# Cross-attention setup: weight and context transposes moved ahead of products on TensorE, block transposes moved ahead of copies on VectorE

## The chip, the cores and the metric

The kernel runs on one core of a Trainium2 chip. The metric is device time in microseconds for one execution. Three runs of the kernel before gave 283.92, 284.35 and 285.65 us, so the median is 284.35 us.

## The reference

One layer of cross-attention, in float32, with 16 batches, 256 queries of width 256, 77 keys of width 192 and 8 heads of width 256:

```
Q = (x @ Wq)   K = (c @ Wk)   V = (c @ Wv)      # split into 8 heads of 256
score = Q K^T / sqrt(256), masked
ctx   = softmax(score) V
out   = ctx @ Wo + x
return layernorm(out) * gamma + beta
```

x is 16 x 256 x 256, c is 16 x 77 x 192, Wq is 256 x 2048, Wk and Wv are 192 x 2048, Wo is 2048 x 256.

## The kernel before

**What it computes instead.** The kernel never forms Q and K. Per head it makes G = Wk Wq^T / 16 once (192 x 256), then A = c G for each batch, and the scores are x A^T. In the same way it makes U = Wv Wo per head once and uses c U in place of V Wo. The 192 rows of Wk and of c are split into 128 (names ending in A: gA, cA, uA) and 64 (gB, cB, uB).

**Order.** The kernel is scheduled by hand: on every engine the instructions stand in the order in which the Python code emits them, and an engine waits where its next instruction isn't ready. There is no planner.

**The setup**, lines 547 to 827, comes before a loop over the batches (line 838). In order of the code:

1. SP issues the loads (lines 574 to 601). The order on its queue is: wk_nat first half, wk_last, wq_nat first half, wk_nat second half, wq_nat second half, the first three row blocks of the context c_sb (load_c(0, first), where first is 3), then the block-wise weights wk_blk and wq_blk for e = 0 and e = 1, the rest of c_sb, wvT, wo, the mask and x.
2. keep_busy (line 606) runs transposes of an identity matrix on TensorE that nothing reads.
3. Half of the heads goes through TensorE transposes. turn_k(e) and turn_q(e, u) (lines 625 to 637) transpose four 128 x 128 chunks each into one PSUM bank, pt, and one copy takes the bank to SBUF (kT, qT). g_of(e) (line 721) multiplies kT and qT into a bank pg, which ScalarE scales into gA. rest_of_g(u) (line 735) does the 64 remaining rows into a bank ph, which VectorE scales into gB.
4. turn_c (line 654) transposes row blocks of the context on TensorE into banks pc and copies them to cA and cB; GpSimd copies cB to the other half of the partitions.
5. turn_blk(e) (line 647) transposes the other half of the heads' weights on VectorE, in 32 x 32 blocks, with one instruction for kT_blk and one for qT_blk. of_pair and rest_of_pairs (lines 679 and 691) multiply these into the banks pgb and phb.
6. a_of_places (line 749) makes A for the first four batches. Its products (lines 199 and 213) fill all eight banks of PSUM (pa), and eight copies take them to SBUF (a).
7. The rest of the setup makes U (banks pu and pw), the bias from the mask, transposed x, and the last 13 keys (banks pr).

**Copies.** evacuate (line 148) gives odd calls to ScalarE and even calls to VectorE, counted over the whole kernel:

```
evacs[0] += 1
if evacs[0] % 2:
    nc.scalar.copy(dst, src)
else:
    nc.vector.tensor_copy(dst, src)
```

**PSUM.** All banks come from one ring of eight (ps_mm, line 98). A new bank can be written once its earlier content has been read.

**The main loop** (lines 838 to 922) does for each batch the scores (line 313), softmax on VectorE, ScalarE and GpSimd, the products with c U, the residual and the normalisation, and prepares A and c U of later batches.

Of the kernel before, what the change touches and what calls it, by code (L numbers as in the profile page):

```python
# [53 lines left out]
def kernel(  # L54
# [81 lines left out]
    def flat(ap):  # L136
        return ap.rearrange("p a b -> p (a b)")
# [10 lines left out]
    def evacuate(dst, src):  # L148
# [5 lines that stand above are left out]
# [395 lines left out]
    with tc.tile_pool(name="wonce", bufs=1) as wp:  # L549
# [23 lines left out]
        first = -(-GB * S2 // CR)  # L573
# [44 lines left out]
        def turn_chunks(of, name):  # L618

            pt = ps_mm.tile([P, 4, P], F32, tag="mm", name=f"pt_{name}")  # L620
            for i, chunk in enumerate(of):
                nc.tensor.transpose(pt[:, i], chunk, ident)
            return pt

        def turn_q(e, u):
            chunks = [
                wq_nat[:, e, t, u * D + dc * P : u * D + (dc + 1) * P]
                for dc in range(2) for t in range(2)
            ]
            pt = turn_chunks(chunks, f"q_{e}_{u}")  # L630
            evacuate(flat(qT[:, e, u]), flat(pt))

        def turn_k(e):
            pt = turn_chunks([wk_nat[:, e, n * P : (n + 1) * P] for n in range(4)], f"k_{e}")
            evacuate(
                kT[:, e].rearrange("p u n l -> p (u n) l")[:, :, :P], pt
            )
# [9 lines left out]
        def turn_blk(e):  # L647
            for blk, of in ((wk_blk, kT_blk), (wq_blk, qT_blk)):
                nc.vector.transpose(
                    of[:, e].rearrange("p n (m r) -> p m n r", r=BK),  # L650
                    blk[:, e].rearrange("p m (n c) -> p m n c", c=BK),
                )

        def turn_c(lo, hi):
            for r in range(lo, hi, 2):
                n = min(2, hi - r)
                pc = ps_mm.tile([P, 4, P], F32, tag="mm", name=f"pc_{r}")
                for lc in range(2):
                    for j in range(n):
                        nc.tensor.transpose(  # L660
                            pc[:, 2 * lc + j, :CR],
                            c_sb[:, r + j, lc * LB : lc * LB + P],
                            ident[:CR, :CR],
                        )
                rows = slice(r * CR, (r + n) * CR)
                evacuate(flat(cA)[:, rows].rearrange("p (j m) -> p j m", m=CR), pc[:, :n, :CR])
                evacuate(
                    flat(cB)[LB:, rows].rearrange("p (j m) -> p j m", m=CR),
                    pc[LB:, 2 : 2 + n, :CR],
                )  # L670
                nc.gpsimd.tensor_copy(flat(cB)[:LB, rows], flat(cB)[LB:, rows])  # L671
# [34 lines left out]
        def two_banks(name, j):  # L706
            return [ps_mm.tile([P, 2, DI], F32, tag="mm", name=f"{name}_{j}_{e}") for e in range(2)]
# [13 lines left out]
        def g_of(e):  # L721

            pg = ps_mm.tile([P, 2, DI], F32, tag="mm", name=f"pg_{e}")
            for u in range(2):
                for dc in range(2):
                    nc.tensor.matmul(
                        pg[:, u],
                        kT[:, e, u, dc, :P],
                        qT[:, e, u, dc],
                        start=(dc == 0),  # L730
                        stop=(dc == 1),
                    )
            nc.scalar.mul(gA[:, NF * e : NF * e + 2], pg, D ** -0.5)

        def rest_of_g(u):

            ph = ps_mm.tile([P, DI], F32, tag="mm", name=f"ph_{u}")
            for dc in range(2):
                for e in range(2):
                    nc.tensor.matmul(  # L740
                        ph[half(e)],
                        kT[:, e, u, dc, P:],
                        qT[:, e, u, dc],
                        start=(dc == 0),
                        stop=(dc == 1),
                    )
            nc.vector.tensor_scalar(gB[:, u], ph, D ** -0.5, None, ALU.mult)

        def a_of_places(places, between=None):
            part_A, part_B, copies = prepare_a(0, places)  # L750
            part_A()
            part_B()
            for i, (dst, src) in enumerate(copies()):
                evacuate(dst, src)
                if between and i == 3:
                    between()

        turn_k(0)
        keep_busy(2)
# [1 line left out]
        keep_busy(3)  # L761
        turn_q(0, 0)
        turn_q(0, 1)
        g_of(0)
        turn_k(1)
        turn_q(1, 0)
        turn_q(1, 1)
        g_of(1)
        rest_of_g(0)
        rest_of_g(1)  # L770
        turn_c(0, first)
        turn_blk(0)
        a_of_places((0, 1), lambda: turn_blk(1))
        pg = two_banks("pgb", 0)
        for e in range(2):
            of_pair(pg, e, wk_part, wq_part)
# [7 lines left out]
        nc.sync.dma_start(gam, gamma.partition_broadcast(P))  # L784
        nc.sync.dma_start(bet, beta.partition_broadcast(P))
        a_of_places((2, 3))
        turn_v(3)
        turn_c(first, NCR)
# [49 lines left out]
    for b in range(-1, B):  # L838
# [32 lines left out]
        copies = [copy for _, _, of_part in work for copy in of_part()]  # L871
# [94 lines left out]
```

## Time and profile before

| what | value |
|---|---|
| runs | 283.92, 284.35, 285.65 us |
| profiled execution | 285.26 us, span 283.5 us |
| granted TensorE clock, mean | 0.992 |
| TensorE matmul busy | 271.2 us (96% of the span) |
| VectorE busy | 207.5 us (73%) |
| GpSimd busy | 179.6 us (63%) |
| ScalarE busy | 156.8 us (55%) |
| DMA | 22.60 MB, mean 80 GB/s |

The span runs from the first to the last instruction of the profiled execution; its own time is 1.76 us longer. PE is TensorE, PEld its weight loads, DVE VectorE, ACT ScalarE, POOL GpSimd, SP the engine that issues the transfers. "pt L622" is the work that writes tile pt in line 622. A float32 matmul appears as two records and a transpose as one, so that the four products of g_of are "x8" and the four transposes of turn_k "x4". In the chain of work that ended last, each piece is what released the next; "issue" is time in which the engine waited for nothing that the profile shows.

| stage (us from the start) | TensorE busy | VectorE busy | ScalarE busy | GpSimd busy | DMA share |
|---|---|---|---|---|---|
| 0 to 17.34 | 14.40 | 3.58 | 5.31 | 0.79 | 0.90 |
| 17.34 to 58.78 | 41.09 | 24.67 | 10.15 | 19.10 | 0.95 |
| 58.78 to 228.70 | 169.92 | 137.56 | 116.15 | 125.37 | 0.17 |
| 228.70 to 283.50 | 45.80 | 41.68 | 25.23 | 34.30 | 0.09 |

### The profile page before, as it was taken

Reading aid. Unit: us, or ns where it says so; the run is one execution under the profiler, and the core shown is the slowest. Engines: PE = TensorE matmul, PEld = TensorE weight load, DVE = VectorE, ACT = ScalarE, POOL = GpSimd, SP = SyncE. Lnnn points to the kernel's source line nnn. Section 1 sums busy time; section 2 is a strip of 40 time slices with the busy share of each in tenths; the row PEclk is TensorE's granted clock in tenths of the full one; section 3 lists DMA queues with packets and bytes.
Section 4 is the critical chain, followed back from the end, with each engine's and each line's share of the span. In section 5 each row is a group of like instructions: output and inputs, shape, how many; then the busy total and the mean of one; then the engine's idle time right before and its main releaser. Section 6 shows DMA issues by size and latency. Waiting matters only on the chain.

```text
span 283.5 us, 13229 instructions
## 1 busy us (share of the span) xinstructions
PE 271.2 (96%) x5925; PEld 196.8 (69%) x5925; DVE 207.5 (73%) x421; ACT 156.8 (55%) x390; POOL 179.6 (63%) x240
## 2 busy tenths in 40 slices
PE   7899999999999999999999999999999999999970
PEld 7756589985585859586858595959595957568440
DVE  0245762678738888878788888787888868898882
ACT  3212142147547676767676767676768834725641
POOL 1000049955677777787877777878777556748574
PEclk9999999999999999999999999999999999999996
DMA  5997899940000000940100009401010101010112
GB/s 186 239 225 170 258 291 232 169 133 3 2 6 2 25 19 27 201 152 3 42 2 28 16 17 214 152 5 41 4 39 4 39 5 39 3 39 5 39 38 74
DMA packets 35640, 22.60 MB, mean 80 GB/s; under 512 B 17712, under 2 KB 34048, under 8 KB 35584
## 3 DMA queue, kind: packets, MB, share of 16 engines
q1 hardware_dynamic: 35584, 21.77, 30.1%
q8 instruction: 46, 0.75, 1.1%
q14 instruction: 10, 0.08, 0.1%
HBM read 17.57 MB, written 4.19 MB: 77 GB/s over the span
## 4 chain that ended last, share of the span: by engine, by line
PE 77%; DVE 11%; POOL 4%; DMA 2%; ACT 2%; issue 2%; POOLq 0%; SPq 0%
PE ps L313 19%; PE pa L199 12%; PE po L436 9%; PE pv L241 7%; PE pm L436 7%; PE pa L213 6%; PE pv L252 4%; PE pu L683 3%; PE pr L274 2%; DMA wq_nat<-in_L_xattn_Wq_dram 2%; DVE top L335 2%; DVE s L328 2%; DVE bn L491 2%; DVE pT L373 2%; POOL p L363 1%
## 5 line engine op out<-in xcount | busy, mean ns | idle before, releaser
L349 ACT ACTIVATE e<-s,top 128x77 f32<-128x77 f32 x192 | 50.3, 346 | 42.9 <-DVE top L335 40.7
L313 PE MATMUL ps<-a,xT 128*32 128x154 f32 x2048 | 70.1, 294 | 0.0
L313 PEld LDWEIGHTS ps<-a,xT 128*32 128x32 f32 x2048 | 66.3, 110 | 1.6 <-issue 0.7
L363 POOL TENSOR_TENSOR p<-e,rden 128x512 f32<-128x512 f32 x64 | 46.7, 752 | 27.3 <-DVE rden L357 24.2
L328 DVE TENSOR_TENSOR s<-ps,bias 128x308 f32<-128x308 f32 x64 | 29.7, 473 | 14.8 <-PE ps L313 13.1
L199 PE MATMUL pa<-cA,gA 128*32 128x308 f32 x512 | 35.9, 423 | 0.4 <-ACT cA L151 0.4
L469 POOL TENSOR_TENSOR xg<-xg,m 128x256 f32<-128x256 f32 x33 | 24.2, 733 | 13.8 <-DVE xg L483 12.1
L199 PEld LDWEIGHTS pa<-cA,gA 128*32 128x32 f32 x512 | 17.0, 110 | 20.5 <-issue 7.0
L241 PE MATMUL pv<-uA,cA 128*32 128x512 f32 x256 | 30.6, 592 | 0.0
L355 DVE TENSOR_REDUCE den<-e 128x8 f32<-128x616 f32 x32 | 24.8, 776 | 7.2 <-ACT e L346 4.8
L373 DVE STREAM_TRANSPOSE pT<-p 128x640 f32<-128x640 f32 x32 | 25.5, 825 | 2.8 <-POOL p L363 2.8
L335 DVE TENSOR_REDUCE top<-s 128x8 f32<-128x616 f32 x32 | 25.4, 795 | 1.1
L671 POOL COPY cB<-cB 64x224 f32<-64x224 f32 (+1 forms) x6 | 1.9, 358 | 37.3 <-DVE cB L153 37.3
L399 POOL TENSOR_TENSOR ts<-vw 128x768 f32<-128x768 f32 x11 | 22.0, 2001 | 0.0
L385 PE MATMUL po<-vw,pT 128*32 128x256 f32 x320 | 19.2, 380 | 0.5 <-DVE pT L373 0.5
L213 PE MATMUL pa<-cB,gB 64*32 64x308 f32 x512 | 19.5, 420 | 0.0
L502 ACT ACT_TABLE_LOAD x15 | 19.2, 1283 | 0.3
L213 PEld LDWEIGHTS pa<-cB,gB 64*32 64x32 f32 x512 | 9.7, 107 | 11.3 <-issue 7.6
L337 POOL TENSOR_TENSOR s<-s,top 128x616 f32<-128x616 f32 x8 | 9.7, 1217 | 12.2 <-DVE top L335 11.0
L252 PE MATMUL pv<-uB,cB 64*32 64x512 f32 x256 | 17.4, 601 | 0.0
L385 PEld LDWEIGHTS po<-vw,pT 128*32 128x32 f32 x320 | 10.3, 110 | 10.0 <-DVE s L328 2.5
L531 DVE SCALAR_TENSOR_TENSOR xg<-xg,mv,gam 128x256 f32<-128x256 f32 x25 | 16.8, 671 | 0.0
(116 smaller groups left out, 474.7 us busy)
## 6 DMA issues: line engine op xcount, KB each, us to landing
xT<-in_x_dram SPq DMA_DIRECT2D x16, 256.0 KB, 5.7
xg<-in_x_dram SPq DMA_DIRECT2D x4, 1024.0 KB, 7.4
out_dram<-xg SPq DMA_DIRECT2D x15, 256.0 KB, 2.4
wo<-in_L_xattn_Wo_dram SPq DMA_DIRECT2D x4, 512.0 KB, 5.4
wvT<-in_L_xattn_Wv_dram SPq DMA_DIRECT2D x16, 96.0 KB, 4.0
wq_nat<-in_L_xattn_Wq_dram SPq DMA_DIRECT2D x2, 512.0 KB, 6.8
wq_blk<-in_L_xattn_Wq_dram SPq DMA_DIRECT2D x8, 128.0 KB, 4.3
wk_blk<-in_L_xattn_Wk_dram SPq DMA_DIRECT2D x8, 96.0 KB, 6.2
```

Source lines behind the costliest of these rows:

```text
L199: nc.tensor.matmul(flat(o[i * BK : (i + 1) * BK]), gA[:, h, cols(dc, i)], flat(cA[:, batches, :]), start=not B_first, stop=B_first,)
L213: nc.tensor.matmul(flat(banks[j + k][i * BK : (i + 1) * BK]), gB[half(k), h % NF, cols(dc, i)], flat(cB[half(k), batches, :]), start=B_fir ...
L241: nc.tensor.matmul(pv[k][i * BK : (i + 1) * BK], cA[:, b, k * BK : (k + 1) * BK], uA[:, parts, :, i], start=True, stop=False,)
L252: nc.tensor.matmul(pv[k][i * BK : (i + 1) * BK], cB[half(k), b, k * BK : (k + 1) * BK], uB[half(k), parts, :, i], start=False, stop=True,)
L313: nc.tensor.matmul(ps[m // 2][i * BK : (i + 1) * BK, m % 2 * 2 * S2 : (m % 2 + 1) * 2 * S2], xT_of[g][:, j * NM + m, dc], flat(a_of[g][:, ...
L328: nc.vector.tensor_tensor(s[:, a * H // 2 : (a + 1) * H // 2], ps[a][:, : H // 2 * S2].rearrange("p (h k) -> p h k", k=S2), bias[:, b, :]. ...
L335: nc.vector.tensor_reduce(top, s, AX.X, ALU.max, negate=t // QT <= NS)
L349: nc.scalar.activation(e[:, h], s[:, h], AF.Exp, bias=top[:, h : h + 1])
L363: nc.gpsimd.tensor_tensor(part, e_mh[:, :, :, keys], rden_mh.unsqueeze(3).to_broadcast(list(part.shape)), ALU.mult,)
L373: nc.vector.transpose(pT_of[t].rearrange("p n m q -> p m n q"), p.rearrange("p m (n k) -> p m n k", k=BK),)
L385: nc.tensor.matmul(po[i * BK : (i + 1) * BK], pT[:, n, i], vw_of[b][:, 2 - n // 2 * 2 : 4 - n // 2 * 2, n % 2, :] if n < NF else vr[:, b, ...
L436: nc.tensor.matmul(out[i * BK : (i + 1) * BK], weight[:, i], moving, start=(n == 0), stop=(n == len(terms) - 1),)
```

## The change

Three moves in the setup. turn_k(1) is emitted before g_of(0) instead of after it. turn_c(0, first) is emitted before g_of(1) instead of after rest_of_g(1). turn_blk(1), which was emitted between the fourth and the fifth copy of A for the places 0 and 1, is emitted right after turn_blk(0), ahead of A's products and copies. The argument by which a_of_places ran something between its copies goes away. Nothing is added or left out.

```diff
-        def a_of_places(places, between=None):
+        def a_of_places(places):
             part_A, part_B, copies = prepare_a(0, places)
             part_A()
             part_B()
-            for i, (dst, src) in enumerate(copies()):
+            for dst, src in copies():
                 evacuate(dst, src)
-                if between and i == 3:
-                    between()
 
         turn_k(0)
         keep_busy(2)
         turn_k_last()
         keep_busy(3)
         turn_q(0, 0)
         turn_q(0, 1)
+        turn_k(1)
         g_of(0)
-        turn_k(1)
         turn_q(1, 0)
         turn_q(1, 1)
+        turn_c(0, first)
         g_of(1)
         rest_of_g(0)
         rest_of_g(1)
-        turn_c(0, first)
         turn_blk(0)
-        a_of_places((0, 1), lambda: turn_blk(1))
+        turn_blk(1)
+        a_of_places((0, 1))
```

## The prediction

> **What bounds the kernel now.** I read the chain that ended last first, in order of time, because only what stands on it sets the end. Columns: start, length, work, all in us.
>
> ```profile
> 1.63 5.63 DMA wq_nat<-in_L_xattn_Wq_dram
> 7.26 0.04 issue
> 7.30 0.67 PE pt_q L622 x4
> 7.97 0.02 issue
> 8.00 0.70 DVE qT L153
> 8.70 0.14 issue
> 8.83 1.96 PE pg L726 x8
> 10.80 0.44 PE pt_k L622 x4
> 11.24 0.45 PE pt_q L622 x4
> 11.69 0.02 issue
> 11.71 0.59 ACT qT L151
> 12.30 0.04 issue
> 12.35 1.99 PE pg L726 x8
> 14.34 1.88 PE ph L740 x16
> 16.22 0.55 PE pc L660 x4
> 16.77 0.02 issue
> 16.79 0.51 ACT cA L151 x2
> 17.30 0.04 issue
> 17.34 4.35 PE pa L199 x64
> ```
>
> The start waits for one weight transfer. From 7.30 the path is TensorE, except in three places where it runs through a copy out of PSUM: qT at 8.00, qT at 11.71, cA at 16.79. The waits of TensorE say what those places cost (engine and line, what it waited for, us, times, longest):
>
> ```profile
> PE pg L726 <- DVE qT L153: 0.4, 1, 0.4
> PE pa L199 <- ACT cA L151: 0.4, 1, 0.4
> PE pg L726 <- ACT qT L151: 0.2, 1, 0.2
> ```
>
> The timeline gives the exact idle times: 0.44, 0.40 and 0.24 us, together 1.08 us. After 17.34 the stages view has TensorE busy 41.09 of 41.44 us up to 58.78, and 169.92 of 169.92 us from there to 228.70. Then a tail of 54.8 us follows in which the chain is mostly VectorE and GpSimd work fed by TensorE. So a microsecond saved before 17.34 moves everything behind it, unless a transfer binds; a microsecond saved on VectorE after 17.34 moves nothing.
>
> **What the Trainium skill says.** "PSUM — Partial Sum Buffer", section "Engine vs sequencer instructions": matmuls start and complete in program order, only weight loads run ahead, and the other engines' queues are strict FIFO. The trace agrees: the weight load of turn_k(1) starts at 10.42, its matmul at 10.63. So a transpose put ahead of a product fills a gap only if its data have landed, and otherwise holds the product back. "DMA: Bandwidth & Descriptors", section "Issuing engines are not separate DMA queues": all transfers run on the same 16 DMA engines and interleave. The trace agrees: 0.90 mean DMA share to 17.34, and c_sb's 252 KB need 8.7 us where the first wk_nat's 256 KB needed 3.4. Each landing must therefore be read off separately. "VectorE: DVE Perf Modes", section "The three transpose paths": TensorE transposes into PSUM, VectorE only 32x32 blocks. Its 390 ns (bf16) I do not use; four here take 0.44 us of the path.
>
> **The landings** (issue start plus time to landing, from the DMA view in short windows): wk_nat second half 2.10 + 6.2 = 8.30; wq_nat second half 2.61 + 8.1 = 10.71; first c_sb 3.09 + 8.7 = 11.79; last piece of wk_blk second half 13.7 + 4.2 = 17.9; of wq_blk second half 16.0 + 4.3 = 20.3.
>
> **The change, part by part.** No instruction is added or removed, and no DMA issue moves on SP. ACT and VectorE still take the evacuations by turns, and since turn_k(1) stays the sixth call and turn_c follows turn_q(1, 1) as before, each copy keeps its engine. The PSUM ring of eight is used in another order, but the same 14 banks precede the A products.
>
> *turn_k(1) ahead of g_of(0).* Four transposes, 0.44 us, begin when turn_q(0, 1) ends. That is 8.39, because the wait of 0.44 ends at 8.83. The data are there at 8.30, by 0.09 us. They end at 8.83 to 8.87, just when qT's copy (8.00 to 8.69) lets pg start. pg(0) keeps its place and ends at 10.80. turn_q(1, 0) then starts at 10.80 instead of 11.24: saved 0.44. Its data landed at 10.71, by 0.09 us. VectorE copies kT at about 8.9 instead of 11.27, in idle time.
>
> *turn_c ahead of g_of(1).* turn_q(1, 0) ends at 11.24, turn_q(1, 1) at 11.69. c_sb is there at 11.79; with the 0.04 us seen between wq_nat's landing and its reader, turn_c begins at 11.83: a new wait of 0.14. Six transposes at 0.11 take 0.66 (4 x 0.11 is the 0.44 above), to 12.49. What is queued behind: pg(1), whose inputs are ready by then. ACT does gA from 10.84 to 11.44, then qT to 12.03; VectorE's qT, which only the second half of pg(1) reads, runs 11.71 to 12.40. So pg(1) starts at 12.49, against 12.35 before. pg and ph take 3.87 us (12.35 to 16.22) and end at 16.36.
>
> *A starts without waiting.* cA's and cB's copies, 0.51 and 0.58 us, begin at about 12.4 and are done by 13.7, behind pg(1). GpSimd's copy of cB moves to about 13, where GpSimd is idle. gA's second scaling (0.60) follows pg at 14.48 and ends by 15.1. So A starts at 16.36 instead of 17.34: 0.98 us. The same by waits: 1.08 removed, less 0.14 new, gives 0.94. I take **0.95**. If the copies were not covered by pg(1), the old 0.40 would be back.
>
> *turn_blk(1) ahead of the copies of A.* VectorE's last gB ends at about 16.85; each pair costs 2.10 us (17.78 to 19.88 before). The first ends at 18.95. The third transpose, 0.97, ends at 19.9; the fourth waits for wq_blk's last piece until 20.33 and ends at 21.53. A's first bank is complete at 22.47 - 0.98 = 21.49. VectorE's four copies so start at about 21.55, where they would anyway. pgb starts when part B ends, at 22.9, with its second bank free at about 22.0. Cost 0; cover about 0.9 us. Gain 0 too: before, pgb's second half ran past 26 and turn_blk(1) was done at 25.51, so it was no wait; the last two A copies, at 25.44 to 26.26, were needed by the products of 30.02.
>
> *Unknown: the stall at 25.00.* The chain shows it in the middle of pgb:
>
> ```profile
> 23.93 1.06 PE pgb L683 x8
> 25.00 0.34 issue
> 25.34 2.86 PE pgb L683 x24
> ```
>
> No releaser is shown. VectorE was transposing the second pair then, but these products read the first. From both sides: it may go (gain 0.34 more) or double (loss 0.34). I take 0.
>
> *Later transfers.* With A early by 0.95: wvT's last piece landed at about 31.9, its transposes began at 30.81 for the first part and 37.13 for the last; wo's first part landed at 34.2, pu will start at 37.3; bias at 40.8, read at 44.84; xT's last part at 40.6 + 5.1 = 45.7, transposed at 52.34. All keep over 2 us, so the saving isn't given back to DMA.
>
> **Sum.** Profiled execution: 285.26, span 283.50, 1.76 around it; after: span 282.55, time 284.3. The three runs' median is 284.35, 0.9 lower than the profiled one; I set the saving against it: 284.35 - 0.95 = **283.4**, 0.33% faster, below the 1% (about 2.8 us) that a measurement of this kernel can tell from no change.
>
> **Rivals.**
> 1. *The transposes meet their transfers* (0.19). Three landings precede their new readers by 0.09 and 0.09 us and follow by 0.10. Against: all three were read off one execution, and turn_k(1) and turn_q(1, 0) were started by a transfer on the same engines, so a general delay moves both. For: the transfers interleave. Each us that c_sb is later costs one; at 0.5 us the saving is 0.45, time 283.9; at 0.95 it is gone, 284.35. Before, c_sb had 16.15 - 11.79 = 4.4 us to spare.
> 2. *Slower: VectorE's queue is held by wq_blk* (0.07). All A copies of VectorE now queue behind the fourth transpose. It decides from a landing at about 22.1 on (1.8 us later than read): then transposes end at 23.3, the first copy at 23.8, and pgb starts no earlier than before. Each further us costs one. The transpose began at 24.31 without a wait before, which bounds the landing: 25.51 + 0.5 gives pgb at 26.0 against 23.86, +2.2, time 286.5. Against: pieces landed within 4.1 to 4.3 us each.
> 3. *The stall of 0.34 goes as well* (0.12): 284.35 - 1.29 = 283.1.
> 4. *The change doesn't do what it says for VectorE*: turn_blk(1) already lay in a hole. I hold this true, so it is in the forecast.
>
> The forecast has 0.62. **How the numbers follow.** The cases span 283.1 to 284.35, with 0.07 above. The runs of before spread from 0.43 below their median to 1.30 above it, so a median can move by about 0.5. Low: 283.1 - 0.5 = 282.6, rounded to 282.5; high: 284.35 + 0.5 = 284.9. Faster by over 1% (below 281.5) needs three times the waits removed: 0.03. Slower by over 1% (above 287.2) needs rival 2 past its bound, or both rivals at once: 0.04. Within 1%: 0.93.
>
> **What would show it.** Right: TensorE's waits for qT and cA gone from its list; pt_k at about 8.4; pc at about 11.8 with a wait of 0.1 to 0.2 for c_sb; first pa at 16.4; pgb at 22.9; the end of the setup (ps L313 at 58.78) at 57.8; the chain from there unchanged. Wrong: a wait of pt_k, pt_q or pc for a DMA of over 0.3 us; pgb waiting for VectorE's copy of a; a first pa at 16.4 with ps at 58.7, which would mean that a transfer or GpSimd took it back.

## The result and the profile after

The changed kernel takes 283.07 us (median of six runs, 282.88 to 283.36), the kernel before 284.42 us (six runs). The ratio is 0.9949, with a 95% interval of 0.9928 to 0.9970: 1.35 us less by the medians, 0.85 to 2.05 us by the interval. The forecast was 283.4, so the time lies in the stated range and on the stated side; the saving was put at 0.95 us. The profiled execution took 282.88 us with a span of 281.1 us.

The chain that ended last, of the changed kernel, in the stretch of the lines shown of before (start, length, work):

```profile
1.61 5.60 DMA wq_nat<-in_L_xattn_Wq_dram
7.21 0.04 issue
7.25 1.09 PE pt_q L622 x8
8.35 0.03 issue
8.38 0.66 PE pt_k L622 x4
9.03 1.73 PE pg L726 x8
10.76 0.87 PE pt_q L622 x8
11.63 0.69 PE pc L660 x6
12.33 1.74 PE pg L726 x8
14.07 1.88 PE ph L740 x16
15.95 4.29 PE pa L199 x64
20.23 2.23 PE pa L213 x64
22.46 3.66 PE pgb L683 x32
```

No copy stands on it any more: from the landing of wq_nat to the end of pgb the chain is TensorE alone. The three waits for qT, qT and cA are gone from the list of TensorE's waits. The whole list is now:

```profile
PE idle L608 <- POOL ident masks.py:199: 1.3, 1, 1.3
PE po L385 <- DVE pT L373: 0.5, 1, 0.5
PE pt_q L622 <- DMA wq_nat<-in_L_xattn_Wq_dram: 0.5, 1, 0.5
```

Chain pieces run from one modelled end to the next, so I also read the starts, from TensorE's timeline of the changed kernel (start, length, work):

```profile
7.25 1.09 PE L622 MATMUL pt_q<-ident,wq_nat 128*128 128x128 f32 x8 [0.52 <-DMA wq_nat<-in_L_xattn_Wq_dram]
8.38 0.66 PE L622 MATMUL pt_k<-ident,wk_nat 128*128 128x128 f32 x4
8.87 1.89 PE L726 MATMUL pg<-qT,kT 128*128 128x256 f32 x8
10.60 1.04 PE L622 MATMUL pt_q<-ident,wq_nat 128*128 128x128 f32 x8
11.56 0.77 PE L660 MATMUL pc<-ident,c_sb 112*128 112x112 f32 x6
12.16 1.91 PE L726 MATMUL pg<-qT,kT 128*128 128x256 f32 x8
14.00 1.95 PE L740 MATMUL ph<-qT,kT 128*64 128x256 f32 x16
15.88 4.36 PE L199 MATMUL pa<-cA,gA 128*32 128x308 f32 x64
```

The same view of the kernel before:

```profile
7.30 1.09 PE L622 MATMUL pt_q<-ident,wq_nat 128*128 128x128 f32 x8 [0.53 <-DMA wq_nat<-in_L_xattn_Wq_dram]
8.83 1.96 PE L726 MATMUL pg<-qT,kT 128*128 128x256 f32 x8 [0.44 <-DVE qT L153]
10.63 0.60 PE L622 MATMUL pt_k<-ident,wk_nat 128*128 128x128 f32 x4
11.07 1.04 PE L622 MATMUL pt_q<-ident,wq_nat 128*128 128x128 f32 x8
12.35 1.99 PE L726 MATMUL pg<-qT,kT 128*128 128x256 f32 x8 [0.24 <-ACT qT L151]
14.27 1.95 PE L740 MATMUL ph<-qT,kT 128*64 128x256 f32 x16
16.15 0.80 PE L660 MATMUL pc<-ident,c_sb 112*128 112x112 f32 x6
17.34 4.35 PE L199 MATMUL pa<-cA,gA 128*32 128x308 f32 x64 [0.40 <-ACT cA L151]
```

The time that each group holds TensorE, from its start to the next group's start, whatever that is in its kernel:

| group | before | after |
|---|---|---|
| first pt_q | 1.53 | 1.13 |
| pt_k | 0.44 | 0.49 |
| first pg | 1.80 | 1.73 |
| second pt_q | 1.28 | 0.96 |
| second pg | 1.92 | 1.84 |
| ph | 1.88 | 1.88 |
| pc | 1.19 | 0.60 |
| first pt_q to first pa | 10.04 | 8.63 |

So the change took 1.41 us out of this stretch. It shows where: the groups that were followed by a wait. The experiments below show what these groups take when nothing holds up the next one: the second pt_q 0.87 us and pc 0.58 us (e4, e6), the first pt_q, which begins after a wait, 0.93 us (e8). Measured by these, the changed kernel still waits twice, and its list of waits has neither: first pt_q has 1.13 - 0.93 = 0.20 us, in which pt_k waits for wk_nat (landed at 2.08 + 6.2 = 8.28, first transpose at 8.38), and second pt_q has 0.96 - 0.87 = 0.09 us, in which pc waits for c_sb (landed at 3.07 + 8.4 = 11.47, first transpose at 11.56).

Spans differ by more, 283.5 - 281.1 = 2.4 us. Beyond the 1.41, 0.05 is the earlier landing of wq_nat, and 0.6 is pgb: between A's last product and phb the chain of before has 1.06 + 0.34 + 2.86 = 4.26 us, the changed one 3.66. The rest, about 0.3 us, is a stall of TensorE at 123 to 126 us in the main loop of the profiled execution of before. The experiments ask whether these belong to the change.

### The profile page after: what moved, and what is told of

Same layout as the page of the kernel before. It is cut to its first block, busy times and chain, and to the rows that moved or that the text cites. A ratio compares the mean times of both kernels' runs of the same rounds, so it can differ in the third digit from the quotient of the medians.

```text
span 281.1 us, 13230 instructions
## 1 busy us (share of the span) xinstructions
PE 270.2 (96%) x5925; PEld 195.8 (70%) x5925; DVE 207.3 (74%) x421; ACT 156.7 (56%) x390; POOL 179.4 (64%) x240
## 4 chain that ended last, share of the span: by engine, by line
PE 78%; DVE 11%; POOL 4%; DMA 2%; ACT 1%; issue 1%; POOLq 0%; SPq 0%
PE ps L313 19%; PE pa L199 12%; PE po L436 9%; PE pm L436 7%; PE pv L241 7%; PE pa L213 6%; PE pv L252 4%; PE pu L683 3%; PE pr L274 2%; DMA wq_nat<-in_L_xattn_Wq_dram 2%; DVE top L335 2%; DVE s L328 2%; DVE bn L491 2%; DVE pT L373 2%; POOL p L363 1%
```

## The experiments

Two theories were set against each other. Theory 1: the two moves on TensorE are the whole gain, and turn_blk(1) is worth nothing. Theory 2: the second pair of blocks, turned by VectorE while pgb runs, caused the stall in pgb, and moving it away is part of the gain. Since wq_nat's landing moved between the profiled executions (first pt_q from 6.80 to 7.51 us), the length from first pt_q to first pa is the yardstick for the first part.

### The parts alone

Both moves on TensorE, turn_blk(1) as before (e1), against the kernel before:

```diff
+        turn_k(1)
         g_of(0)
-        turn_k(1)
         turn_q(1, 0)
         turn_q(1, 1)
+        turn_c(0, first)
         g_of(1)
         rest_of_g(0)
         rest_of_g(1)
-        turn_c(0, first)
```

> Both moves on TensorE (turn_k(1) ahead of g_of(0), turn_c ahead of g_of(1)), turn_blk(1) left between the copies of A. Theory 1, the moves on TensorE are the whole gain and turn_blk(1) is worth nothing: the first product of A starts at 15.9 us (before 17.34, after 15.88), the scores start at 56.7 to 57.3 us and the time is that of the changed kernel, about 1.3 us below before. Theory 2, turning the second pair of blocks while pgb runs causes the stall seen in the middle of pgb in the profile of before: pgb lasts 4.2 us here, not 3.7, and only about 0.8 us of the gain is left.

Measured: 282.85 us against 284.43, ratio 0.9951 (0.9936 to 0.9966), the whole gain. pgb lasts 3.73 us with the blocks turned beside it. So theory 1 holds and theory 2 falls. First pa was expected at 15.9 and came at 16.26 in the profiled execution, which took 283.70 us and shows the first rival of the prediction at work:

```profile
7.04 1.09 PE L622 MATMUL pt_q<-ident,wq_nat 128*128 128x128 f32 x8 [1.07 <-DMA wq_nat<-in_L_xattn_Wq_dram]
8.56 0.66 PE L622 MATMUL pt_k<-ident,wk_nat 128*128 128x128 f32 x4 [0.43 <-DMA wk_nat<-in_L_xattn_Wk_dram]
9.05 1.89 PE L726 MATMUL pg<-qT,kT 128*128 128x256 f32 x8
10.78 1.07 PE L622 MATMUL pt_q<-ident,wq_nat 128*128 128x128 f32 x8
11.94 0.77 PE L660 MATMUL pc<-ident,c_sb 112*128 112x112 f32 x6
```

The transposes meet their transfer: wk_nat landed at 2.08 + 6.4 = 8.48 us, and pt_k, with pg behind it, waited 0.43 us for it. pc starts 1.16 us after pt_q, 0.20 later than in the changed kernel, with c_sb landed at 3.07 + 8.7 = 11.77 us. From first pt_q to first pa it is 9.22 us here, 0.59 more than in the changed kernel: 0.39 at pt_k and 0.20 at pc.

Only turn_blk(1) moved (e2):

```diff
         turn_blk(0)
-        a_of_places((0, 1), lambda: turn_blk(1))
+        turn_blk(1)
+        a_of_places((0, 1))
```

> Only turn_blk(1) moved ahead of the copies of A. Theory 1: no wait of TensorE is removed, the first product of A stays at 17.3 us, the time stays within 0.3 us of before. Theory 2: pgb shrinks from 4.27 to 3.66 us and the time falls by about 0.6 us.

Measured: 284.34 us against 284.43, ratio 0.9997 (0.9987 to 1.0007). From first pt_q to first pa 10.04 us, as before, and TensorE's three waits for copies unchanged. pgb lasts 3.72 us in its profile, yet the median over 14 runs stays where it was: the move is worth nothing that shows, at most 0.13% by the interval.

Only turn_k(1) moved (e3), and only turn_c moved (e4):

```diff
+        turn_k(1)
         g_of(0)
-        turn_k(1)
```

> Only turn_k(1) moved ahead of g_of(0). Theory 1: TensorE's wait of 0.44 us for qT goes, q's transposes start at 10.6 instead of 11.07 us, the waits for the second qT (0.2 to 0.3) and for cA (0.4) stay, the first product of A starts at about 16.85 us, 0.45 to 0.5 us earlier, and the time falls by as much. Rival, the move only shifts the wait to the next copy because ScalarE is busy with gA when q is transposed: the first product of A stays at 17.2 to 17.3 us.

```diff
         turn_q(1, 1)
+        turn_c(0, first)
         g_of(1)
         rest_of_g(0)
         rest_of_g(1)
-        turn_c(0, first)
```

> Only turn_c moved ahead of g_of(1). Theory 1: the waits of 0.24 us for qT and 0.40 us for cA go, the first product of A starts at 16.4 to 16.5 us, 0.85 to 0.95 us earlier, and the time falls by as much; with turn_k(1) alone this adds up to the 1.46 us seen with both. Rival, c_sb's landing holds turn_c: TensorE waits for a DMA ahead of the context's transposes (which start at about 12.0 here, so there is none under theory 1).

Measured, e3: 284.06 us, ratio 0.9994 (0.9984 to 1.0004). The interval holds no change at all, though the median of its 21 runs is 0.37 us lower; from first pt_q to first pa 9.73 us, 0.31 less than before, where 0.45 to 0.5 was expected. e4: 283.27 us, ratio 0.9960 (0.9947 to 0.9972); 8.93 us, 1.11 less, where 0.85 to 0.95 was expected. 0.31 + 1.11 = 1.42: the parts add up to the 1.41 of both. TensorE's timeline of e4 also gives the groups back to back, since c_sb had landed at 3.07 + 8.0 = 11.07 us, ahead of pc:

```profile
11.07 1.04 PE L622 MATMUL pt_q<-ident,wq_nat 128*128 128x128 f32 x8
11.94 0.74 PE L660 MATMUL pc<-ident,c_sb 112*128 112x112 f32 x6
12.52 1.91 PE L726 MATMUL pg<-qT,kT 128*128 128x256 f32 x8
```

pt_q holds TensorE for 0.87 us and pc for 0.58. The timeline of e3 tells why its part is small:

```profile
7.00 1.09 PE L622 MATMUL pt_q<-ident,wq_nat 128*128 128x128 f32 x8
8.19 0.66 PE L622 MATMUL pt_k<-ident,wk_nat 128*128 128x128 f32 x4
8.69 1.89 PE L726 MATMUL pg<-qT,kT 128*128 128x256 f32 x8
10.41 1.04 PE L622 MATMUL pt_q<-ident,wq_nat 128*128 128x128 f32 x8
11.74 1.99 PE L726 MATMUL pg<-qT,kT 128*128 128x256 f32 x8 [0.29 <-ACT qT L151]
```

pt_q is done with TensorE 0.93 us after its start, at 7.93, but pt_k starts at 8.19, when wk_nat (2.10 + 6.1, about 8.2) has landed; pg then starts 1.69 us after pt_q instead of 1.53. And the wait for the second qT is still there, 0.29 instead of 0.24 us: ScalarE has gA to scale first. This much of the rival was right.

### The same kernels once more

Before, unchanged (e5), and after, unchanged (e6), one execution each:

> The kernel before, unchanged, profiled once more. Theory 1, the stall of 0.34 us inside pgb and the one of 0.17 us at 125 us belong to that one execution: pgb lasts about 3.7 us here and the span is 282.6 to 283.2 us. Theory 2, the stall comes from the second pair of blocks being turned at that time: pgb lasts 4.2 us again. Under both the first product of A starts at 17.2 to 17.4 us.

> The changed kernel, unchanged, profiled once more, for the spread of the landings: c_sb, wq_nat and wk_nat land within 0.4 us of the first profile (11.5, 10.2 and 8.3 us), the first product of A starts at 15.8 to 16.2 us, pgb lasts 3.7 us. If the transposes do meet their transfers, TensorE shows a wait for a DMA of over 0.1 us ahead of pt_k, pt_q or pc.

Measured, e5: 284.51 us, span 282.7. From first pt_q to first pa 10.04 us. pgb has no stall this time, though VectorE turns the second pair at 23.61 as it runs:

```profile
24.05 3.73 PE L683 MATMUL pgb<-qT_blk,kT_blk 64*128 64x256 f32 x32
```

So the placing of the blocks alone does not bring the 0.34 us. Of seven profiles with the blocks turned beside pgb two have the stall (before and e9, both after pgb's ninth weight load), of four with the blocks turned ahead of it none (after, e2, e6 and e10; in e7, below, pgb waits for something else); that is too few to say that the placing makes it likelier, and e2's times say that it is worth nothing. Stalls come and go elsewhere too: 0.5 us at 123 us in e2, 0.3 us at 122 us in e4, both without anything in the trace that they wait for. What causes them stays open; it was not tried.

e6: 282.63 us. From first pt_q to first pa 8.66 us against 8.63; as pt_q started at 6.80, first pa came at 15.46, earlier than the 15.8 to 16.2 expected. wk_nat landed at 8.0, wq_nat at 2.60 + 7.1 = 9.7 and c_sb at 10.7 us. Of the landings 0.4 us of spread was expected; the first keeps within it, the others come 0.5 and 0.8 us earlier than in the first profile. pt_k waits 0.2 us for wk_nat by the view and 1.28 - 0.93 = 0.35 us by the starts, so the new wait is there again. Second pt_q is followed by pc after 0.87 us and pc by pg after 0.58, as in e4: with c_sb this early there is no wait for it.

### What a gap costs

Four transposes that nothing reads, in the gap ahead of the first pg of the kernel before (e8):

```diff
         turn_q(0, 1)
+        keep_busy(4)
         g_of(0)
```

> The kernel before with four transposes of the identity matrix, which nothing reads, put in the gap ahead of g_of(0); nothing is moved and nothing is left out. Theory, a gap costs TensorE more than its idle time, because the next group's first products otherwise start in the drain of the group before: g_of(0) still starts at about 8.85 us but the next transposes start about 0.1 us earlier (10.55 instead of 10.63 us). Rival, a gap costs its idle time alone: they start at 10.63 us or later. The time can't tell these apart; the timeline can.

Measured: 284.24 us in its one run. Its timeline:

```profile
7.20 1.09 PE L622 MATMUL pt_q<-ident,wq_nat 128*128 128x128 f32 x8 [0.32 <-DMA wq_nat<-in_L_xattn_Wq_dram]
8.13 0.60 PE L608 MATMUL idle<-ident 128*128 128x128 f32 x4
8.73 1.97 PE L726 MATMUL pg<-qT,kT 128*128 128x256 f32 x8
```

The filler follows pt_q after 0.93 us, which is what pt_q takes when nothing holds up the next group. pg starts 1.53 us after pt_q, and pt_k 1.81 us after pg (1.80 before): filling the gap gave nothing, though the idle time of 0.44 us is gone from the list of waits. (Four transposes take 0.44 us from start to start, so the last 0.16 us ahead of pg stayed empty.) That pt_k stands at 10.54 is only because pt_q started at 7.20. The theory that a refilled gap also speeds up the next group fell here, for a group that still starts when its copy ends. What shortens first and second pg by 0.07 to 0.08 us in the changed kernel is only argued: there the weight loads of pg start 0.09 to 0.11 us ahead of its first product, here 0.03.

### What the transfers cost now

The first context load issued after four pieces of wk_blk, in the kernel before (e9) and in the changed one (e10):

```diff
-        load_c(0, first)
         for e in range(2):
             load_blocks(wk_blk[:, e], wk_blocks[2 * e + 1])
+            if e == 0:
+                load_c(0, first)
             load_blocks(wq_blk[:, e], wq_blocks[2 * e + 1])
```

> The kernel before with the first context load issued after the four pieces of wk_blk's first half instead of ahead of them; nothing is left out. c_sb then lands 1.5 to 2.5 us later, at about 13 to 14 us. Theory, before had 4.4 us to spare at this load: TensorE doesn't wait for it, the first product of A comes 10.0 us after the first transpose of q as before, and the time stays within 0.3 us of before.

> The changed kernel with the same late context load. Theory, the change has put the load's landing on the path: TensorE waits 1.5 to 2.5 us for c_sb ahead of turn_c, g_of(1) is held behind it, the first product of A comes 10.2 to 11.1 us after the first transpose of q instead of 8.6, and the time is 284.6 to 285.5 us, at or above the kernel before. Rival, the saving holds because the work behind turn_c has slack: 8.6 us and 283.1 us as in the changed kernel.

Measured, e9: 284.56 us against 284.69, ratio 0.9996 (0.9983 to 1.0010); from first pt_q to first pa 10.05 us; c_sb landed at 5.88 + 7.5 = 13.4 us and nobody waited. e10: 284.98 us against 284.69, ratio 1.0014 (0.9994 to 1.0033), the gain gone; its 20 runs spread from 283.79 to 287.92 us. Its timeline:

```profile
10.34 1.04 PE L623 MATMUL pt_q<-ident,wq_nat 128*128 128x128 f32 x8
12.91 0.77 PE L661 MATMUL pc<-ident,c_sb 112*128 112x112 f32 x6 [1.53 <-DMA c_sb<-in_ctx_dram]
13.51 1.91 PE L727 MATMUL pg<-qT,kT 128*128 128x256 f32 x8
15.35 1.95 PE L741 MATMUL ph<-qT,kT 128*64 128x256 f32 x16
17.22 4.36 PE L199 MATMUL pa<-cA,gA 128*32 128x308 f32 x64
```

c_sb landed at 5.20 + 7.6 = 12.80 us, 0.6 us earlier than in e9. TensorE waited 1.53 us, and pg, whose own inputs were ready, stood behind it. From first pt_q to first pa it is 10.16 us. The same delay that before had room for costs the changed kernel all it won: the change spent 4.4 us of room at this load.

The rest of the context ahead of the last four pieces of wq_blk, in the changed kernel (e7):

```diff
             load_blocks(wk_blk[:, e], wk_blocks[2 * e + 1])
+            if e:
+                load_c(first, NCR)
             load_blocks(wq_blk[:, e], wq_blocks[2 * e + 1])
-        load_c(first, NCR)
```

> The changed kernel with the rest of the context (672 KB) loaded ahead of the last four pieces of wq_blk, so that these land later; nothing is left out. Theory, VectorE's copies of A queue behind the fourth block transpose and have only about 0.25 us of cover (in the profile of the changed kernel the first copy ends at about 22.2 us and pgb starts at 22.4): the pieces land 2 to 3 us later, the transposes end at about 24 to 25 us, pgb starts at 24.5 to 25.5 us instead of 22.4, and the time rises by 2 to 3 us to about 285 to 286 us. Rival, VectorE is off the path here: pgb stays at 22.4 us and the time at 283.1 us.

Measured: 283.85 us, ratio to before 0.9972 (0.9960 to 0.9985). VectorE waits 3.94 us for wq_blk and its copies of A come at 25.03, as expected, but pgb does not wait for them. VectorE and weight loads of e7:

```profile
23.02 1.60 PEld L684 LDWEIGHTS pgb<-qT_blk,kT_blk 64*128 64x128 f32 x16 [0.50 <-ACT a L151]
...
23.86 1.25 DVE L650 STREAM_TRANSPOSE qT_blk<-wq_blk 128x1024 f32<-128x1024 f32 x1 [3.94 <-DMA wq_blk<-in_L_xattn_Wq_dram]
25.03 1.60 DVE L153 COPY a<-pa 128x308 f32<-128x308 f32 x4
25.16 1.60 PEld L684 LDWEIGHTS pgb<-qT_blk,kT_blk 64*128 64x128 f32 x16 [0.54 <-DVE qT_blk L650]
```

pgb starts at 23.02, ahead of every copy of A on VectorE: its first products write both of its banks, so ScalarE, which alone had copied by then, had freed both. Only its second half waits, for the transposed blocks themselves, and it lasts 4.13 us instead of 3.73. So a landing late by 3 us cost 0.4 us here, not 2 to 3; the theory put the gate in the wrong place. The other part of the loss, in this execution, is a wait of 0.51 us for c_sb, which landed at 12.1 us (from first pt_q to first pa 9.34 us); its load was issued at 3.08 us as ever. How much of the median's loss it is, one profile can't say.

## Why the prediction was right, step by step

**The bound.** Right. The chain up to pgb is now TensorE alone, and the saving came through to the end: the scores start 2.08 us earlier in the profile (58.78 to 56.70; 1.46 of it at first pa, the rest the stall in pgb of before), and the time fell by 1.35 us. No transfer and no GpSimd work took it back.

**turn_k(1).** The mechanism was right, the size not. It was put at 0.44 us, with the data there 0.09 us ahead of the reader. By starts, pt_q leaves TensorE at 7.30 + 0.93 = 8.23 in the profile of before, and wk_nat landed at 8.30. So the margin was none and a wait for wk_nat arises. It is there in all six profiles with this move: pt_k starts 1.04 to 1.52 us after pt_q, where 0.93 would do. That pt_k started at 8.38, where 8.4 was forecast, is luck: it started then because wk_nat had just landed, not because pt_q had just ended. The move alone is worth 0.31 us.

**turn_c.** The mechanism was right, the size not. A wait of 0.14 us for c_sb was expected; by starts it is 0.09 us in the changed kernel, none in e4 and e6, more in e1 and e7. Alone the move is worth 1.11 us, where its waits of 0.24 and 0.40 less 0.14 made 0.50.

**The sum.** This is the term that was mis-sized: 1.08 us of waits removed. The idle time that the view gives begins at the modelled end of the last matmul, but the next group could have started before that end. By starts, the waits of before are 1.53 - 0.93 = 0.60, 1.28 - 0.87 = 0.41 and 1.19 - 0.58 = 0.61, together 1.62 us instead of 1.08. Less the new waits, 0.20 for wk_nat and 0.09 for c_sb, less 0.05 at pt_k and 0.02 at pc, plus 0.07 + 0.08 at the two pg, this is 1.41, as measured. The forecast used the chain's pieces, which have the same modelled ends. So two errors ran against each other, 0.54 us too little removed and 0.15 too little added (0.29 instead of 0.14), and that the forecast lies within 0.4 us of the time owes something to luck. The profiled execution, forecast at 284.3 us, took 282.88: here the stalls of before, about 0.6 and 0.3 us, are gone besides.

**turn_blk(1) at nothing.** Right (e2), and VectorE waited for wq_blk as foreseen: until 20.64, foreseen 20.33. But "with its second bank free" by a copy of VectorE was wrong: e7 shows that pgb needs none of these copies.

**The rivals.** The first, the transposes meeting their transfers, is real: the views of e1, e6 and e7 list such waits of 0.43, 0.2 and 0.51 us without any delay to these loads put in, two of them over the 0.3 us that the prediction named as a sign, and e10 shows that a landing at 12.8 us takes the gain away. It did not decide the median. The second, slower through VectorE's queue, named the wrong gate: not the copies of A but pgb's second half, at 0.4 us for a landing 3 us late. The third, the stall gone as well, is what the two profiles show, but e5 has no stall either, without the change.

## What to carry to other kernels

Take what a wait costs an engine from start to start, against the same group running back to back, not from the idle time of the view; for TensorE here the two differ by 0.54 us over three waits, and two waits for transfers of 0.20 and 0.09 us are missing from the list. A transpose moved ahead into a gap must have its data: compare its new start with the landing in several executions, since it holds everything behind it if it is late. And fill a gap only with work that has to be done; filler that nothing reads left the groups behind it where they were.

## What the runs showed of the hardware

Landings differ between executions of the same loads by more than the margins that the change works with. wq_nat's first half was in use from 6.80 us (e6) to 7.51 us (e9). The first c_sb, issued at 3.07 to 3.09 us in all kernels but e9 and e10, landed between 10.7 us (e6) and 12.1 us (e7). In a row, eight float32 transposes of 128 x 128 hold TensorE for 0.87 us, 0.11 us each (e4, e6); eight that begin after a wait hold it for 0.93 us (e8). TensorE also stalls now and then inside a run of products, by 0.3 to 0.5 us, at the same places of the program (in pgb, and in the products at 122 to 126 us) in some executions and not in others, with nothing in the trace to wait for; the cause stays open.
